# A planner's list of TensorE durations set to traced values, and fillers kept to longer gaps

## The chip, the cores and the metric

The kernel runs on one core of one Trainium2 chip. The metric is the device time of one execution in microseconds; a run's time is that of its slowest core, which here is the only one.

## What is computed

An image batch of shape 8 x 256 x 32 x 32 (8 samples, 256 channels, 1024 positions) goes through four layers:

- Layer 0: a channel norm; attention with 4 heads (key width 32, head width 64) over the 1024 positions; a 3x3 depthwise term and a projection; then a feed-forward part with 1024 hidden channels, 3x3 depthwise convolutions, a gated GELU and a product in the frequency domain of 8x8 patches.
- Layer 1: group norm, attention with 8 heads of width 32 over the same positions, a projection, group norm and a small MLP.
- Layer 2: three convolutions (1x1, 3x3, 1x1) with fake quantization, an addition and a last quantization to codes of 8 bits.
- Layer 3: a selective scan (Mamba) in four directions over the 1024 positions.

The attention of both layers is, cut to what matters:

```
attn = softmax(q^T k * scale)        # 1024 x 1024 for each sample and head
out  = attn applied to v
```

The kernel first needs, for each query, the maximum and the sum of exponentials over 1024 keys. Then it recomputes the scores, subtracts the logarithm of the sum, takes the exponential and multiplies by the values.

## The kernel before

`phase_a` holds layers 0 to 2, `phase_b` holds layer 3. Every operation of both is written as a small object (`_Op`) that a generator, called a strand, yields. Nothing is issued when it is yielded. A planner, `_Order`, holds all strands and keeps a clock of its own for each engine (`order.free`). It repeatedly takes the strand whose next item could start first by that clock (`start`), breaking ties by rank, issues the item and moves the engine's clock on by the item's cost (`run`). A signal between two engines is put at 0.35 us (`LATENCY`). So the order of instructions on every engine is the planner's, and the planner's costs set it. The chip then executes each engine's list in that order; the costs are not seen again.

A strand may yield one operation, a list of operations of one engine that stay together, or a pair of a cost and such a list. `go` turns these into a cost: the operation's own, the sum over the list, or the number that was given. An operation's own cost is in `_Op.__init__`; a float32 matmul with 512 columns costs 1.76 x 0.5 = 0.88 us.

In phase A eight samples go through layers 0 to 2 as one strand each (`sample`), of which about three are under way at once. Each starts further strands:

- `maxima`: two strands (`some`) take two or four PSUM banks at a time, issue two or four score matmuls with 32 rows each that share TensorE's rows, and then for each bank a maximum on VectorE (`tensor_reduce`) and an exponential with a sum on ScalarE. The matmuls are yielded with a cost of 0.9 for two and 1.0 for four.
- `exponentials`: its strands (`step`) take four banks, issue four score matmuls and four with one row block of -1 (`minus`) that subtract the logarithms, at a cost of SCORES = 1.3; ScalarE then takes four exponentials, after each of which a bank comes free. `values` multiplies them by the values, at a cost of 0.9 x (4n/128), where n is 64 in layer 0 and 32 in layer 1: 1.8 and 0.9.
- All other matmuls of the layers (`mm` and the like) are yielded singly or as lists with the sum of their own costs.

There are eight PSUM banks (`bank`) in phase A. While a sample is in `exponentials`, other work may hold three of them (`OTHERS`). DMAs are issued from SP's queue.

Fillers: ahead of each TensorE item `run` calls `fill` with the item's planned start. `fill` looks how long TensorE is free by the plan before that start, counted from when a bank for it is free, and issues one dummy matmul (bf16, constant operands, 512 columns) for each FILL = 0.3 us of that gap. The result is overwritten. A filler goes to a free bank, or to the bank that the next item starts afresh. Fillers have no cost in the plan. They are on the profile's line L1075; all planned operations are on L132, the line of `emit`.

Phase B has a planner of its own, an `_Order` made anew, without fillers.

Of the kernel before, what the change touches and what calls it, by code (L numbers as in the profile page):

```python
# [29 lines left out]
P = 128  # L30
# [138 lines left out]
class _Order:  # L169
# [7 lines left out]
    def __init__(self, nc):  # L177
        self.nc, self.strands, self.n = nc, [], 0
        self.free, self.written, self.read, self.base, self.last = {}, {}, {}, {}, {}
        self.fill = None  # L180

    def add(self, rank, strand):
        self.n += 1
# [4 lines left out]
    def go(self, s, value=None):  # L188
        try:
            r = s[1].send(value)  # L190
            if isinstance(r, _Op):
                r = (r.cost, [r])
            elif isinstance(r, list):
                r = (sum(o.cost for o in r), r)
            s[2] = r
        except StopIteration:
            self.strands.remove(s)
# [63 lines left out]
def phase_a(ctx, tc, i, col, ident, codes):  # L261
# [18 lines left out]
    order = _Order(nc)  # L280
# [249 lines left out]
    def maxima(rank, q, k, rows, done):  # L530

        both = yield from take(stats)
        least, sums = both[:, 0], both[:, 1]
        todo = [(t, j, h) for t in range(NT) for j in range(2) for h in (0, 2)]
        left = [MAXIMA]

        def some():
            while todo:
                yield lambda: not todo or may(2)
                if not todo:  # L540
                    break
                n = 4 if may(4) and not todo[0][2] else 2
                t, j, h = todo.pop(0)
                if n == 4 and todo:
                    todo.pop(0)
                bb = yield from some_banks(n)
                ops = []
                for e in range(n):
                    r = slice(32 * (h + e), 32 * (h + e) + 32)
                    ops.append(  # L550
                        T.matmul(bb[e], lhsT=q[r, t * P : (t + 1) * P], rhs=k[r, hs(j)], start=True, stop=True)
                    )
                yield (0.9 if n == 2 else 1.0, ops)
                for e in range(n):
                    m, s = (x[:, j, t, h + e : h + e + 1] for x in (least, sums))
                    yield V.tensor_reduce(m, bb[e], AX.X, ALU.max, negate=True)
                    yield A.activation(bb[e], bb[e], AF.Exp, bias=m, accum_out=s)
                    back(bb[e])
            left[0] -= 1

        for _ in range(MAXIMA):
            order.add((1, rank), some())
        yield lambda: left[0] == 0 and not making
        making.append(1)
        m, mx, t = (small.tile([P, NT, 4], F32, name=f"mx{e}", tag=f"mx{e}", bufs=2) for e in range(3))
        yield V.tensor_tensor(m, least[:, 0], least[:, 1], ALU.min)
        for j in range(2):
            yield V.tensor_tensor(least[:, j], m, least[:, j], ALU.subtract)
        yield A.activation(least, least, AF.Exp)
        yield V.tensor_tensor(sums, sums, least, ALU.mult)  # L570
        yield V.tensor_tensor(t, sums[:, 0], sums[:, 1], ALU.add)

        y = small.tile([P, NT, 4], F32, name="ln", tag="ln", bufs=2)
        put(stats, both)
        yield A.activation(y, t, AF.Ln)
        yield V.tensor_tensor(mx, y, m, ALU.subtract)
        yield A.activation(y, y, AF.Exp, scale=-1.0)
        yield V.tensor_tensor(t, t, y, ALU.mult)
        yield V.scalar_tensor_tensor(mx, t, -1.0, mx, ALU.add, ALU.add)
        for e in range(2):  # L580
            b = small.tile([P, NT, 4], BF16, name="mb", tag="mb", bufs=2)
            yield V.tensor_copy(b, mx)
            yield V.tensor_copy(parts[:, :, :, e], b)
            yield V.tensor_tensor(mx, mx, parts[:, :, :, e], ALU.subtract)
        yield V.tensor_copy(parts[:, :, :, 2], mx)
        for h in range(2):
            pr = yield from side()
            yield [
                T.transpose(pr[:, t * P : (t + 1) * P], parts[:, 4 * h + t].rearrange("p a b -> p (a b)"), ident)
                for t in range(4)  # L590
            ]
            yield A.copy(rows[:, hs(h)], pr)
            back(pr)
        making.clear()
        done()

    def exponentials(rank, tasks, vt, n, finish):

        yield lambda: not attending
        attending.append(1)
        for task, (h, steps) in enumerate(tasks):
            po = yield from take(bank)
            seen = [0]

            def step(k, four, h=h, seen=seen):
                bb = yield from takes(4, bank, when=lambda: seen[0] >= k - 1)
                ops = []
                for b, (q, kk, rows, key, r, *_) in zip(bb, four):  # L610
                    r4, r3 = slice(r, r + 32), slice(r, r + 3)
                    ops.append(
                        T.matmul(
                            b, lhsT=kk[r4, key * P : (key + 1) * P], rhs=q[r4, hs(h)],
                            start=True, stop=False, skip_group_check=True,
                        )
                    )
                for b, (q, kk, rows, key, r, *_) in zip(bb, four):
                    r3 = slice(r, r + 3)
                    ops.append(  # L620
                        T.matmul(
                            b, lhsT=minus[r3, :], rhs=rows[r3, hs(h)], start=False, stop=True, skip_group_check=True
                        )
                    )
                yield (SCORES, ops)
                tiles = []
                for n in range(2):
                    t = yield from take(exps)
                    for e in range(2):
                        yield A.activation(t[:, e], bb[2 * n + e], AF.Exp)  # L630
                        put(bank, bb[2 * n + e])
                    tiles.append(t)
                order.add((1, rank), values(k, four, tiles))

            def values(k, four, tiles, po=po, seen=seen, last=len(steps) - 1):
                es = [t[:, e] for t in tiles for e in range(2)]
                yield lambda: seen[0] == k
                ops = []
                for e, (q, kk, rows, key, r, c, at) in zip(es, four):
                    ops.append(  # L640
                        T.matmul(
                            po[at : at + n], lhsT=vt[:, key, c : c + n], rhs=e,
                            start=(k == 0 and key == 0), stop=(k == last), skip_group_check=True,
                        )
                    )
                yield (0.9 * (4 * n // P), ops)
                for t in tiles:
                    put(exps, t)
                seen[0] += 1

            for k, four in enumerate(steps):
                order.add((0, rank), step(k, four))
            yield lambda: seen[0] == len(steps)
            order.add((0, rank), finish(task, po))
        attending.clear()
# [397 lines left out]
    def fill(gap, ops):  # L1053


        free, o = order.free.get("tensor", 0.0), ops[0]
        spare = min(bank.left, key=lambda k: order.last.get((bank.tag, k), 0.0), default=None)
        own = o.method == "matmul" and o.kw["start"] and o.args[0].shape[-1] == HALF and o.kw["rhs"].shape[0] > 3
        since = min(
            [order.last.get((bank.tag, k), 0.0) for k in bank.left] + [order.base.get(o.args[0].name, 0.0)] * own,  # L1060
            default=1e9,
        )
        n = int((gap - max(free, since)) / FILL)
        if n < 1:
            return
        if spare is not None and order.last.get((bank.tag, spare), 0.0) <= since:
            bank.left.remove(spare)
            bank.left.insert(0, spare)
            t = bank.take()
        else:  # L1070
            t = None
        out = o.args[0] if t is None else t
        rhs = minus.unsqueeze(1).to_broadcast([P, 4, P])
        for _ in range(n):
            nc.tensor.matmul(out, lhsT=minus[:, : out.shape[0]], rhs=rhs, start=True, stop=True)  # L1075
        if t is not None:
            bank.put(t)

    order.fill = fill
    stage = [0] * B  # L1080

    def sample(b):
# [640 lines left out]
```

## Time and profile before

| what | value |
|---|---|
| runs | 10776.5, 10775.12, 10765.92 us; median 10775.12 |
| profiled execution, its own time | 10771.94 us |
| its span | 10770.2 us |
| mean granted TensorE clock | 0.957 |
| fillers (matmuls on L1075) | 1594, from 1.6 to 3666.7 us |
| ScalarE, exponentials of scores (`exps`) | 1536, 797.4 us busy, mean 621 ns |
| ScalarE, exponentials of maxima (`bank`) | 1536, 1023.0 us busy, mean 669 ns |
| VectorE, maxima (`stats`) | 1536, 981.5 us busy, mean 681 ns |
| VectorE, waiting in front of the maxima for TensorE's banks | 746.4 us |

The span runs from the first to the last instruction; the execution's own time is 1.7 us longer. In rows of the timeline the first number is the start in microseconds, the second the time that the merged instructions took, and "x4" how many there were. A float32 matmul that isn't a transpose appears as two records, so "x8" is four matmuls. In rows of the windows, the columns are the stretch, its length, the busy time of TensorE, its weight loads, VectorE, ScalarE and GpSimd with the count of instructions, the mean granted TensorE clock, the busy share of the DMA engines, and GB/s. Tiles are named without buffer numbers: `bank` is a PSUM bank, `exps` an exponential, `big` a buffer with q, k, v or the like, `minus` a constant of -1.

### The profile page before, as it was taken

The page shows a single profiled execution, that of the slowest core. Times are in us where ns is not written, and L with a number is a line of the kernel's source. Part 1 is how long each engine was busy: PE and PEld are TensorE (multiplying, and loading weights), DVE is VectorE, ACT ScalarE, POOL GpSimd, SP SyncE. Part 2 cuts the span into 40 slices and gives each one's busy share as a digit, 9 for nine tenths or more (in the row PEclk, how much of TensorE's full clock was granted, in tenths as well). Part 3 has the DMA queues.
Part 4 walks back from the last instruction along what each step waited for, and adds up shares of the span by engine and source line. Part 5 has one row for each costly group of instructions (what it writes and reads, how often), then busy time and mean ns, then how long its engine had stood idle before and what let it go on. Part 6 is the DMA issues. An engine that isn't in the chain of part 4 may idle for free. (4 is left out here: it accounts for less than half of the span.)

```text
span 10770.2 us, 157247 instructions
## 1 busy us (share of the span) xinstructions
PE 9924.2 (92%) x58586; PEld 6252.6 (58%) x58698; DVE 8478.2 (79%) x8992; ACT 8690.8 (81%) x16283; POOL 6733.0 (63%) x3745
## 2 busy tenths in 40 slices
PE   9999999999999889999999999999989999999998
PEld 3333333333333267777777777777777777777776
DVE  5266557577665379898998998998899899899897
ACT  7867676777767488888888888888888888888887
POOL 1432133132220178888888888888888888888887
PEclk7988999989999899999999999999999999999999
DMA  1000000000000011111111111111111111111111
GB/s 46 29 18 16 22 16 22 13 22 12 13 13 10 30 41 39 50 48 50 48 46 52 50 41 55 41 50 53 44 49 52 47 48 46 52 50 43 55 41 47
DMA packets 217345, 410.00 MB, mean 38 GB/s; under 512 B 24881, under 2 KB 69297, under 8 KB 211458
## 3 DMA queue, kind: packets, MB, share of 16 engines
q1 hardware_dynamic: 216578, 399.94, 12.0%
q8 instruction: 461, 7.55, 0.3%
q14 instruction: 306, 2.51, 0.1%
HBM read 358.43 MB, written 30.93 MB: 36 GB/s over the span
## 5 line engine op out<-in xcount | busy, mean ns | idle before, releaser
L132 POOL TENSOR_TENSOR h<-h,cb 128x1024 f32<-128x1024 f32 x2048 | 4873.9, 2395 | 899.6 <-ACT st L132 445.5
L132 ACT ACTIVATE da<-dt,am 128x512 f32<-128x512 f32 x4096 | 2869.3, 713 | 505.9 <-DVE h L132 497.4
L132 DVE TENSOR_TENSOR_SCAN h<-da,st,db 128x512 f32<-128x512 f32 x2048 | 2467.2, 1257 | 167.9 <-PE db L132 92.7
L132 DVE TENSOR_TENSOR_SCAN h<-da,db 128x512 f32<-128x512 f32 x2048 | 2346.1, 1198 | 230.7 <-PE db L132 152.0
L132 ACT ACTIVATE dbu<-du,bT 128x512 f32<-128x512 f32 x3584 | 2474.9, 709 | 34.1 <-PE db L132 31.8
L132 PE MATMUL db<-ident,dbu 128*128 128x128 f32 x14336 | 2219.6, 280 | 165.0 <-DVE h L132 134.6
L132 PE MATMUL py<-ident,h 128*128 128x128 f32 x16384 | 2121.1, 275 | 93.9 <-POOL h L132 86.2
L132 PEld LDWEIGHTS db<-ident,dbu 128*128 128x128 f32 x14336 | 1672.9, 143 | 694.4 <-DVE h L132 364.2
L132 PEld LDWEIGHTS py<-ident,h 128*128 128x128 f32 x16384 | 1842.4, 141 | 171.5 <-POOL h L132 140.7
L132 DVE TENSOR_REDUCE stats<-bank 128x1 f32<-128x512 f32 x1536 | 981.5, 681 | 747.5 <-PE bank L132 746.4
L132 ACT ACTIVATE bank<-bank,stats 128x512 f32<-128x512 f32 x1536 | 1023.0, 669 | 391.2 <-DVE stats L132 380.9
L132 POOL TENSOR_TENSOR mid<-mid,mid 128x961 f32<-128x961 f32 (+2 forms) x192 | 401.2, 2097 | 1046.9 <-ACT mid L132 676.9
L132 PE MATMUL pp<-xi,cvd 128*128 128x512 f32 x2048 | 953.3, 609 | 9.6 <-ACT xs L132 3.4
L132 PE MATMUL bank<-big,big 32*128 32x512 f32 x4096 | 908.5, 670 | 36.5 <-ACT bank L132 17.9
L132 ACT ACTIVATE exps<-bank 128x512 f32<-128x512 f32 x1536 | 797.4, 621 | 137.6 <-PE bank L132 133.2
L132 PE MATMUL db<-dg,du 128*128 128x128 f32 x4096 | 811.0, 280 | 0.0
L132 POOL TENSOR_TENSOR dt<-dt,tmp 128x512 f32<-128x512 f32 x512 | 652.0, 1273 | 173.8 <-DVE tmp L132 151.0
L132 DVE TENSOR_TENSOR tmp<-dt,xs 128x512 f32<-128x512 f32 x256 | 604.2, 2360 | 194.3 <-POOL dt L132 194.1
L132 PEld LDWEIGHTS db<-dg,du 128*128 128x128 f32 x4096 | 638.0, 197 | 0.0
L132 PEld LDWEIGHTS pp<-xi,cvd 128*128 128x128 f32 x2048 | 380.8, 196 | 406.4 <-issue 391.9
L132 DVE SCALAR_TENSOR_TENSOR mid<-mid,cols,mid 128x961 f32<-128x961 f32 (+1 forms) x384 | 603.7, 1572 | 6.7
L132 PEld LDWEIGHTS bank<-big,big 32*128 32x128 f32 x4096 | 284.7, 192 | 499.2 <-issue 247.9
(186 smaller groups left out, 11280.3 us busy)
## 6 DMA issues: line engine op xcount, KB each, us to landing
cb<-c_d SPq DMA_DIRECT2D x1024, 256.0 KB, 3.2
wi<-w_in SPq DMA_DIRECT2D x192, 192.0 KB, 3.4
big<-in_x_dram SPq DMA_DIRECT2D x16, 1024.0 KB, 5.6
kept<-big SPq DMA_DIRECT2D x16, 1024.0 KB, 4.0
big<-kept SPq DMA_DIRECT2D x16, 1024.0 KB, 4.9
cdb<-codes SPq DMA_DIRECT2D x48, 256.0 KB, 4.1
big<-big SPq DMA_DIRECT2D x16, 512.0 KB, 7.2
out_dram<-z SPq DMA_DIRECT2D x32, 256.0 KB, 2.5
```

Source lines behind the costliest of these rows:

```text
L132: return getattr(getattr(nc, self.engine), self.method)(*self.args, **self.kw)
```

## The change

It has four parts, all in the planner's data.

1. Maxima: the matmuls are yielded with 1.06, for two as for four banks.
2. Values: the cost is 0.88 x (4n/128) + 0.12, so 1.88 in layer 0 and 1.00 in layer 1.
3. Lists of TensorE operations that come without a given cost get 0.1 us more (`order.way`, 0.1 in phase A, 0.0 in phase B). Single matmuls and items with a given cost don't.
4. `fill` takes 0.35 us off the gap before it divides by 0.3.

```
-        self.fill = None
+        self.fill, self.way = None, 0.0
...
-                r = (sum(o.cost for o in r), r)
+                r = (sum(o.cost for o in r) + self.way * (r[0].engine == "tensor"), r)
...
-                yield (0.9 if n == 2 else 1.0, ops)
+                yield (1.06, ops)
...
-                yield (0.9 * (4 * n // P), ops)
+                yield (0.88 * (4 * n // P) + 0.12, ops)
...
-        n = int((gap - max(free, since)) / FILL)
+        n = int((gap - max(free, since) - 0.35) / FILL)
...
-    order.fill = fill
+    order.fill, order.way = fill, 0.1
```

## The prediction

> **What bounds the kernel now.** I read the page first, to find which part of the span the edits can touch.
>
> ```profile
> span 10770.2 us, 157247 instructions
> PE 9924.2 (92%) x58586; PEld 6252.6 (58%) x58698; DVE 8478.2 (79%) x8992; ACT 8690.8 (81%) x16283; POOL 6733.0 (63%) x3745
> ...
> PE   9999999999999889999999999999989999999998
> ...
> PEclk7988999989999899999999999999999999999999
> ```
>
> Every slice has TensorE busy, so the page alone decides nothing. The granted clock is lower in the first third than after it, and the groups of the fillers' line say where that third ends and what is in it:
>
> ```profile
> L1075 PE MATMUL bank<-minus x1594: 376/379/634, 1.6 to 3666.7; 128*128 128x512 bf16 x193, 128*64 128x512 bf16 x7
> ```
>
> The last of 1594 fillers starts at 3666.7 us. What follows is phase B, some 7,100 us; its planner has no filler and an extra of 0.0. In the two programs as built its instruction order is the same (common tails of 39,555 TensorE, 10,565 ScalarE and 5,740 VectorE instructions). So it moves as a block, and the change is worth what the first 3667 us change.
>
> Inside those I took the TensorE timeline of a stretch that repeats one pattern, then ScalarE's in the same place:
>
> ```profile
> 1060.23 0.61 PE L1075 MATMUL bank<-minus 128*128 128x512 bf16 x2
> 1060.76 1.14 PE L132 MATMUL bank<-big,big 32*128 32x512 f32 x8
> 1061.72 0.40 PE L132 MATMUL bank<-low,minus 3*128 3x512 bf16 x4
> 1062.05 1.07 PE L132 MATMUL bank<-exps,big 128*32 128x512 f32 x8
> 1063.05 1.13 PE L132 MATMUL bank<-big 32*128 32x512 f32 x4
> 1064.11 0.61 PE L1075 MATMUL bank<-minus 128*128 128x512 bf16 x2
> 1064.64 1.14 PE L132 MATMUL bank<-big,big 32*128 32x512 f32 x8
> ```
>
> ```profile
> 1062.14 2.06 ACT L132 ACTIVATE exps<-bank 128x512 f32<-128x512 f32 x4 [0.73 <-PE bank L132]
> 1064.06 0.70 ACT L132 ACTIVATE bank<-bank,stats 128x512 f32<-128x512 f32 x1
> 1064.99 0.66 ACT L132 ACTIVATE bank<-bank,stats 128x512 f32<-128x512 f32 x1
> 1066.02 2.06 ACT L132 ACTIVATE exps<-bank 128x512 f32<-128x512 f32 x4 [0.25 <-PE bank L132]
> ```
>
> Read starts against starts, since matmul ends are modelled. One step takes 3.88 us (1060.76 to 1064.64): scores with their minus rows 1.29, values 1.00, two maxima 1.06, two fillers 0.53. No row has an idle figure, and ScalarE waits for TensorE's banks. The old plan has 1.3, 0.9 and 0.9 for the three real pieces: it sees a hole that the chip fills with real work, and puts fillers into it. Windows over this stretch and three neighbours show the clock's side:
>
> ```profile
> core 0: us, PE busy (x) PEld busy (x) DVE busy (x) ACT busy (x) POOL busy (x), PEclk, DMA share, GB/s
> 934.00:944.00 10.00, 9.54 (x33) 3.52 (x30) 7.96 (x13) 9.38 (x22) 6.40 (x4) 1.00 0.01 2
> 944.20:957.70 13.50, 13.34 (x25) 4.12 (x24) 6.23 (x10) 9.93 (x27) 6.60 (x4) 0.50 0.00 0
> 958.00:988.00 30.00, 29.22 (x98) 10.79 (x98) 28.89 (x42) 25.08 (x71) 0.00 (x0) 1.00 0.00 0
> 1048.00:1100.00 52.00, 52.00 (x349) 14.71 (x345) 18.84 (x40) 45.82 (x108) 2.53 (x2) 1.00 0.00 1
> ```
>
> The clock is either whole or 0.50. The same view in windows of 400 us gives phase A's level (two of nine rows):
>
> ```profile
> 0.00:400.00 400.00, 376.18 (x1470) 131.83 (x1470) 160.59 (x303) 309.29 (x668) 108.75 (x62) 0.85 0.14 40
> 1200.00:1600.00 400.00, 373.88 (x1734) 125.78 (x1736) 254.41 (x326) 310.96 (x661) 112.34 (x54) 0.95 0.07 23
> ```
>
> From 1048 to 1100 TensorE is full and ScalarE is at 45.82 of 52.00 us, 88%: TensorE binds there, fillers included, with ScalarE 12% behind.
>
> **What the Trainium skill says.** TensorE: Matmul & The Clock Gate, Part 1, has the array at half rate by default and at full rate after about 3.4 us of activity; the trace agrees on the two rates (1.00 and 0.50). Its section Why this matters for your kernels allows idle gaps up to about 3 us. The trace is stricter: summing streaming time in steps of 3.4 us, I find 34 of the 59 drops in phase A after a step that was still 60 to 85% used, and steps above 85% followed by none. Back-to-back issue gap (Part 2) gives 512/2.4 + 2.5 = 216 ns for a 512-column matmul; here a lone filler costs 0.32 us (1532.34 to 1532.66) and a pair 0.53, so each further one costs 0.21: agreed. Perfetto Trace Analysis, Identifying the Most-Contended Engine, warns that matmul occupancy is no measure of headroom; the 52.00 of 52.00 above, a seventh of it fillers, is a case.
>
> **The change part by part.** *Costs.* Maxima become 1.06 (trace 1063.05 to 1064.11: 1.06). Values of layer 1 become 1.00 (trace 1.00), of layer 0 1.88 (trace 254.26 to 256.13: 1.87). A list of two 128-row matmuls goes from 1.76 to 1.86 (trace 1514.49 to 1516.40: 1.91). All move towards the trace. The edits cost the chip nothing themselves; they act by the order and by the gaps that the filler sees. The order on every engine differs from its first few dozen instructions on. The real work is the same, but maxima in fours rise from 97 to 111 and in twos fall from 574 to 546. Four row-packed matmuls take no longer than two (1.06), so 14 groups fewer free 14 x 1.06 = 15 us of TensorE. No wait is written in; those that the dependences need are about as many (TensorE 13,820 and 13,775, ScalarE 14,686 and 14,764). No DMA is added, and SP's count is unchanged; a moved DMA is hidden as before (DMA is 3 to 14% busy here); were that cover gone, one load is 5 us.
>
> *Fillers.* The program before has 1594 in 453 runs, the one after 949 in 243. At 0.32 for the first of a run and 0.215 for others that is 453 x 0.32 + 1141 x 0.215 = 390 us against 243 x 0.32 + 706 x 0.215 = 230 us: 160 us of TensorE issue go. Not all of it stood in the way. For each of the 453 runs I compared its start with the end of the last instruction that frees a bank or makes an input for the group after it, plus 0.15 us for the signal. 97 runs (196 fillers) began when that group was ready; they cost 67 us. With the other runs whose group came before the fillers' end, all fillers together delayed real work by 137 us. That is the ceiling of removal. The steps of the pattern above (four values, two maxima, nothing else) lose most: 129 fillers in 86 steps become 27 in 91.
>
> How much of 137 goes? In the pattern a step falls from 3.88 to at best 3.35 on TensorE, and ScalarE needs 4 x 0.477 + 2 x 0.67 = 3.25 (starts in dense runs), with its small operations 0.88 x 3.88 = 3.4: about 0.45 of 0.53 comes out, and then ScalarE is next. But 11 full-clock steps of this kind that have no filler average 4.0 us (least 3.59), so not every step will reach that. I take 60% of 137: 82 us, plus about two thirds of the 15 us of grouping: 10 us.
>
> *Threshold.* A planned gap under 0.65 us now stays empty, and longer ones keep 0.35 us: where the gap is real, idle TensorE. By the nine windows of 400 us to 3600 the clock was 0.85, 0.90, 0.93, 0.95, 0.93, 0.91, 0.95, 0.91, 0.93, so 0.74 x 400 x 2 = 592 us ran at half rate. TensorE is over 90% busy, so a half-rate microsecond costs about 0.45. Bounds: none more (dropped fillers sat in false gaps) to +300 us (half as much again), that is 0 to 135 us of loss. A gain is possible too, if a denser order leaves fewer thin steps: perhaps 30 us. I take +60 us at half rate: 27 us lost.
>
> Sum: -82 - 10 + 27 = -65 us. On the profiled execution 10771.94 - 65 = 10707; the median of the runs is 3.2 us above it, so 10710 us.
>
> **Rivals.** *The clock (slower).* The 0.35 us left open makes enough 3.4 us steps thin that half rate spreads. It beats the 92 us of gain from about 205 us of new half-rate time on, an average clock of 0.89 where it was 0.92. At +330 us it loses 150 us: 10775 - 92 + 150, about 10835. For it: steps just above the limit are common, and fillers are what lifts them. Against it: where fillers were false, TensorE stays full without them.
>
> *ScalarE and the bank ring (no change).* Freed TensorE time turns into waiting for banks, as in the 4.0 us steps without fillers: of 82 us some 30 remain, the clock takes 25 back: about 10770.
>
> *A better plan (more).* With planned and real times in step, the new order also removes waits that are not fillers: TensorE was idle 174 us in the first 3600 (sum of the same windows). All 137, 15 and a fifth of that idle time: 10775 - 187, about 10590 to 10640.
>
> That the edits do nothing is excluded: the programs differ in 645 matmuls.
>
> **How the numbers follow.** Forecast case (10650 to 10753) 0.53; better plan (below 10650) 0.08; no change (10754 to 10797) 0.17; clock (above) 0.22. A measurement of this kernel tells about 0.2%, 21 us, from none. Faster 0.61, same 0.17, slower 0.22. The range leaves out some 0.08 below 10640 and 0.11 above 10830, the far half of the clock case; the forecast's own is 10650 to 10753.
>
> **What would show it.** After: fillers 949; phase A's last matmul at about 3600; the pattern step at 3.4 to 3.6 us with ScalarE over 92% in it; phase B as long as before; mean clock in phase A 0.90 to 0.92. Wrong if the step still takes 3.9 us with idle TensorE before the scores (no change), or if the clock falls under 0.89 there (slower).

## The result and the profile after

The changed kernel takes 10732.95 us, the median of 5 runs from 10712.72 to 10736.98; the kernel before takes 10775.12 beside it (5 runs, 10751.72 to 10783.01). The ratio is 0.9961, with a 95% interval from 0.9946 to 0.9976: 42 us faster, where 65 were forecast; by the interval the gain is 26 to 58 us. The page of the changed kernel:

```profile
span 10735.2 us, 155993 instructions
PE 9872.1 (92%) x57941; PEld 6286.0 (59%) x58053; DVE 8489.3 (79%) x8995; ACT 8687.5 (81%) x16280; POOL 6739.8 (63%) x3742
...
PE   9999998999999789999999989999999999999997
...
PEclk7988998999898899999999999999999999999999
...
L132 DVE TENSOR_REDUCE stats<-bank 128x1 f32<-128x512 f32 x1536 | 985.7, 684 | 711.8 <-PE bank L132 710.4
```

The engines' busy shares are the same to a per cent, so they would not show that anything happened. VectorE's wait for TensorE's banks ahead of the maxima is 710.4 us, 36 less than before. The fillers' line (min, median and longest duration in ns, then the first and last start) tells where the time went:

```profile
L1075 PE MATMUL bank<-minus x949: 376/379/634, 1.6 to 3617.8; 128*128 128x512 bf16 x178, 128*64 128x512 bf16 x12
```

The last filler starts 49 us earlier. From here on "phase A" is the time to the last matmul that writes a `bank`, read to within a microsecond: 3667.3 us before, 3618.6 after. Phase B's main part, from its first `db` matmul to the end, is the same instructions in both: 6961 and 6976 us, and 6958 to 6976 in all 14 profiles of this study. So a phase's length in one profile moves by some 10 us either way without any change of the kernel. Part of that goes with the clock, whose time at half rate after phase A ranges from 287 to 379 us in these profiles. The 35 us between the two spans are 49 gained in phase A less 14 of such scatter.

The TensorE timeline of the changed kernel, in a stretch with the step of the forecast:

```profile
1568.89 0.39 PE L1075 MATMUL bank<-minus 128*128 128x512 bf16 x1
1569.21 1.18 PE L132 MATMUL bank<-big,big 32*128 32x512 f32 x8
1570.17 0.43 PE L132 MATMUL bank<-low,minus 3*128 3x512 bf16 x4
1570.54 1.06 PE L132 MATMUL bank<-exps,big 128*32 128x512 f32 x8
1571.53 1.13 PE L132 MATMUL bank<-big 32*128 32x512 f32 x4
1572.21 1.31 PE L132 MATMUL bank<-big,big 32*128 32x512 f32 x7
...
1576.03 0.39 PE L1075 MATMUL bank<-minus 128*128 128x512 bf16 x1
1576.35 1.14 PE L132 MATMUL bank<-big,big 32*128 32x512 f32 x8
```

Two steps take 7.14 us (1569.21 to 1576.35), 3.57 each, with one filler for both; before, one took 3.88 with two fillers. From 1571.53 to 1572.21 is less than the 1.06 us that two maxima take elsewhere: they and the next scores even overlap. The stretch shown is better than the mean. Over all such steps at full clock (four scores, four values, two maxima and nothing else but fillers), the mean is 3.89 us in 55 before and 3.62 us in 60 after. That is some 16 us in all, a third of the gain; the rest lies elsewhere. The windows say who is next:

```profile
core 0: us, PE busy (x) PEld busy (x) DVE busy (x) ACT busy (x) POOL busy (x), PEclk, DMA share, GB/s
1562.30:1584.00 21.70, 21.70 (x151) 7.50 (x149) 7.21 (x13) 20.95 (x50) 0.00 (x0) 1.00 0.00 1
```

ScalarE is at 20.95 of 21.70 us, 97%, where it was at 88%. The clock's side, two rows of the windows of 400 us:

```profile
0.00:400.00 400.00, 376.13 (x1467) 143.34 (x1469) 175.26 (x313) 324.92 (x693) 127.35 (x70) 0.84 0.14 40
1200.00:1600.00 400.00, 380.14 (x1639) 132.23 (x1639) 255.90 (x316) 321.39 (x686) 107.33 (x51) 0.91 0.07 23
```

The nine windows to 3600 us give 0.84, 0.91, 0.87, 0.91, 0.92, 0.92, 0.92, 0.93 and 0.93, a mean of 0.906 where it was 0.918. By the clock records phase A ran 692.9 us at half rate; before it was 587.1.

### The profile page after: what moved, and what is told of

It reads as the page before. It is cut to its first block, busy times and chain, and to the rows that moved or that the text cites. A ratio compares the mean times of both kernels' runs of the same rounds, so it can differ in the third digit from the quotient of the medians.

```text
span 10735.2 us, 155993 instructions
## 1 busy us (share of the span) xinstructions
PE 9872.1 (92%) x57941; PEld 6286.0 (59%) x58053; DVE 8489.3 (79%) x8995; ACT 8687.5 (81%) x16280; POOL 6739.8 (63%) x3742
## 5 line engine op out<-in xcount | busy, mean ns | idle before, releaser
L132 DVE TENSOR_REDUCE stats<-bank 128x1 f32<-128x512 f32 x1536 | 985.7, 684 | 711.8 <-PE bank L132 710.4
L132 PE MATMUL bank<-big,big 32*128 32x512 f32 x4096 | 981.1, 684 | 42.5 <-ACT bank L132 37.6
L132 PEld LDWEIGHTS bank<-big,big 32*128 32x128 f32 x4096 | 335.9, 196 | 523.9 <-issue 199.5
L132 POOL TENSOR_SCALAR big<-big,ga,gs 128x512 f32<-128x512 f32 x64 | 63.0, 997 | 909.8 <-DVE gs L132 686.3
```

The source lines that it names most:

```text
L132: return getattr(getattr(nc, self.engine), self.method)(*self.args, **self.kw)
```

## The experiments

The change mixes two things: another order (from the durations) and fewer fillers (from the threshold, and because the new plan has fewer gaps). My theory was that dropped fillers, those in false gaps (gaps of the plan that the chip does not have), give the gain and the clock takes part of it back. The rivals were that the new order gives it, or that fillers hardly matter. Two numbers are read from each trace. "Half rate" is the time in phase A at a granted clock of 0.5. "Delay" is the sum over all runs of fillers of how long they kept the group of matmuls after them waiting when its banks and inputs were ready (with 0.15 us allowed for the signal): 137 us before, 75 after.

### One order, three filler counts

The first two kernels keep the old order, instruction for instruction, and change only how many fillers `fill` issues: those that the new rule leaves, or none.

```
old_order_fewer, in the kernel before:
-        for _ in range(n):
+        for _ in range(int((gap - max(free, since) - 0.35) / FILL)):
old_order_none, in the kernel before, and new_order_none, in the changed kernel:
-        for _ in range(n):
+        for _ in range(0):
costs_only, in the changed kernel:
-        n = int((gap - max(free, since) - 0.35) / FILL)
+        n = int((gap - max(free, since)) / FILL)
```

`costs_only` and `new_order_none` have the changed kernel's order in the same way, but for the numbers of the banks.

Every ratio below is to the kernel before as it was timed beside that kernel, on the same chip. Its median was 10778.04 us beside the four kernels here, 10783.33 beside `way_011`, `scores_129`, `act_cost` and `tight_fill`, and 10774.48 beside the last four further on. So ratios can be compared across the tables, and medians only roughly. Phase A, half rate and delay come from one profiled execution of each kernel.

old_order_fewer: 

> The old order on every engine, instruction for instruction, with the fillers that the new rule leaves: 1102 instead of 1594. If the dropped fillers stood in the way (forecast), this alone gives about half of the change's gain: 10745 us. If the gain is the new order's, this gains nothing, and loses through the clock: 10775 to 10795 us, with over 640 us at half rate in the layers before the scan, where the kernel before had 587.

costs_only: 

> The new durations without the new threshold: the order of the changed kernel (bank numbers apart), with 1373 fillers instead of 949. If the order carries the gain, it is as fast as the changed kernel or faster, 10715 to 10735 us, with less time at half rate than 693 us. If the fillers that the threshold drops stand in the way, it keeps half of the gain: 10750 us.

new_order_none: 

> The order of the changed kernel with no fillers. If fillers hold the clock, half rate before the scan rises from 693 to 900 us or more and the time to 10780 to 10830 us. If they mostly delay work (75 us of delay by the trace after), it falls to about 10690 us.

old_order_none: 

> The order of the kernel before with no fillers. If fillers hold the clock: half rate from 587 to 950 us or more, which costs about 165 us against at most 137 us of delay that goes: 10790 to 10850 us. If they mostly delay: 10690 us.

| kernel | order | fillers | phase A, us | half rate, us | delay, us | median, us | ratio (95%) |
|---|---|---|---|---|---|---|---|
| before | old | 1594 | 3667.3 | 587.1 | 137 | 10775.12 | 1 |
| old_order_fewer | old | 1102 | 3633.6 | 692.9 | 69 | 10740.05 | 0.9961 (0.9947 to 0.9975) |
| old_order_none | old | 0 | 3661.9 | 1097.9 | 0 | 10768.58 | 0.9992 (0.9983 to 1.0001) |
| costs_only | new | 1373 | 3622.3 | 553.0 | 107 | 10729.82 | 0.9956 (0.9939 to 0.9972) |
| after | new | 949 | 3618.6 | 692.9 | 75 | 10732.95 | 0.9961 (0.9946 to 0.9976) |
| new_order_none | new | 0 | 3641.9 | 1043.9 | 0 | 10747.75 | 0.9971 (0.9961 to 0.998) |

The fillers' lines of the two kernels with one part each:

```profile
L1075 PE MATMUL bank<-minus x1102: 376/379/634, 1.6 to 3632.5; 128*128 128x512 bf16 x175, 128*64 128x512 bf16 x9
```

```profile
L1075 PE MATMUL bank<-minus x1373: 376/379/634, 1.6 to 3621.7; 128*128 128x512 bf16 x187, 128*64 128x512 bf16 x10
```

What follows:

- Fewer fillers in the old order are as good as the whole change (0.9961 both). Nothing moved in that kernel but fillers, so it is shown that in this order fillers stood in the way. I had expected about half of the gain from it.
- The durations alone are as good as the whole change too (0.9956), which is the reading that I had set down for the order. The two parts don't add up: the new durations already take out part of the false gaps (1373 fillers, delay 107), and the threshold in the new order gains 3.7 us of phase A, within the scatter. So in the changed kernel's own order no run shows that the 424 fillers dropped by the threshold were worth anything in all; what they gave and cost there is worked out below.
- Without fillers the clock falls. Two rows of `old_order_none`, and the same two of the kernel before:

```profile
1600.00:2000.00 400.00, 353.88 (x1388) 141.70 (x1388) 264.80 (x378) 282.83 (x616) 111.47 (x56) 0.84 0.06 20
2000.00:2400.00 400.00, 353.21 (x1366) 145.70 (x1359) 264.69 (x348) 258.88 (x559) 113.58 (x56) 0.87 0.05 18
```

```profile
1600.00:2000.00 400.00, 376.10 (x1601) 144.22 (x1597) 270.28 (x384) 281.24 (x613) 111.79 (x56) 0.93 0.06 20
2000.00:2400.00 400.00, 370.99 (x1555) 140.06 (x1556) 264.98 (x348) 265.68 (x574) 112.05 (x56) 0.91 0.05 18
```

0.93 becomes 0.84 and 0.91 becomes 0.87, and yet the kernel is no slower: 511 us more at half rate cost what 137 us of delay had cost. My expectation of 10790 to 10850 us was wrong; so was 10780 to 10830 for the new order, which came out at 10747.75.

Two prices explain the three lengths of the old order. Let a microsecond of delay cost a, and one at half rate b. From `old_order_fewer`, -33.7 = -69a + 105.8b; from `old_order_none`, -5.4 = -137a + 510.8b. Hence a = 0.81 and b = 0.21 with the delays before rounding (0.80 and 0.20 with the rounded ones). Two equations for two unknowns leave nothing over to test them with, and 5 us of scatter in each length would move a by up to 0.15 and b by up to 0.05. For the new order, counted from `costs_only`, they give +3 us for the changed kernel (measured -4) and +15 for `new_order_none` (measured +20): within the scatter of one profile.

The record holds a second price, and it is higher. Executions of one unchanged kernel differ in their granted clock, and time goes with it: in the 35 of the kernel before with the median 10774.48, a mean clock of 0.960 went with 10750 us (6 executions) and one of 0.956 with 10784 (3). A line through all 35 gives 0.34 us for each microsecond at half rate, and through the 26 with the median 10778.04 it gives 0.36. That is a correlation over the whole span. It can't replace 0.21 here: with 0.35 the old order would need a = 1.02 in the first equation and 1.34 in the second. So half-rate time that missing fillers cause was cheap in this phase, and 0.21 is no price of the clock in general. Why the two differ is open.

### Other draws of the order

A planner of this kind reorders nearly everything when one number moves. So the order's share may be luck: one draw, so to say, out of many orders. Four of these kernels change a cost that hardly matters, in the changed kernel or in the one before. Two take one part of the durations alone. `act_cost` sets one more number to the trace, and `tight_fill` tries the two prices on the order that is already known.

```
way_011, in the changed kernel:
-    order.fill, order.way = fill, 0.1
+    order.fill, order.way = fill, 0.11
scores_129, in the changed kernel; old_scores_129 and old_scores_131, in the kernel before:
-    MAXIMA, SCORES = 2, 1.3
+    MAXIMA, SCORES = 2, 1.29            (1.31 in the last)
act_cost, in the changed kernel:
-            self.cost = 0.05 + 0.87 * n + (0.1 if len(ins) > 1 else 0)
+            self.cost = 0.05 + 0.87 * n + (0.1 if len(ins) > 1 else 0) + (0.09 if "accum_out" in kw else 0)
tight_fill, in the changed kernel:
-    FILL = 0.3
+    FILL = 0.215
maxima_only: the change's first part alone, old threshold
lists_only: the change's third part alone, old threshold
```

way_011: 

> The changed kernel with 0.11 instead of 0.1 for lists: durations as true as before, another order from the 111th TensorE instruction on, 880 fillers. If the new order's share of the gain comes from true durations, the layers before the scan stay within 10 us of 3619. If it is one draw among many orders, they may end anywhere within some 40 us, up to where they were, 3667 us.

scores_129: 

> The changed kernel with 1.29 instead of 1.3 for the scores (1.29 is what the trace shows): a second draw, 985 fillers. Same two readings: within 10 us of 3619 before the scan, or anywhere up to 3667.

act_cost: 

> The changed kernel with 0.09 us more for each exponential with a sum: planned 0.585, starts in dense runs are 0.67 apart in the trace. If a truer plan pays by itself, this gains again: 3600 us before the scan, 10715 us in all. If what paid was that false gaps went, it gains nothing more: within 10 us of the changed kernel or of its neighbours.

tight_fill: 

> The order of the changed kernel (bank numbers apart); a gap still loses 0.35 us, but what is left is filled at 0.215 us a filler, as the trace has them, not 0.3: 1502 fillers. By the four runs before, a microsecond of delay by fillers costs 0.81 and one at half rate 0.21. If that holds: half rate falls from 693 to about 580 us (gain 24 us) and delay rises from 75 to about 100 us (loss 20 us): no change, 3610 to 3622 us before the scan. If the number of fillers is what costs, it loses 30 us.

old_scores_129: 

> The kernel before with 1.29 instead of 1.3 for the scores: the old durations and the old rule in another order (from the 461st TensorE instruction on), 1695 fillers. If the order of the kernel before was one bad draw, the layers before the scan end well below 3667 us, at 3620 to 3640. If the old durations cost time in any order, they end within 12 us of 3667.

old_scores_131: 

> The kernel before with 1.31 for the scores: a second draw with the old durations, 1641 fillers. Same two readings: 3620 to 3640 us before the scan if the order before was a bad draw, within 12 us of 3667 if the old durations cost time in any order.

lists_only: 

> Of the new durations only the 0.1 us for lists; old rule, 1506 fillers, of which 172 in 105 steps of the common kind (before 129 in 86). The false gaps of these steps remain, so by the forecast's reading this gains little: 3650 to 3670 us before the scan. If the gain is from a truer plan of the other matmuls, 3630 us.

maxima_only: 

> Of the new durations only the maxima's; old rule, 1462 fillers, of which 132 in 97 steps of the common kind. Values are still planned 0.1 short, so false gaps remain in part: 3640 to 3660 us before the scan. If the maxima's cost is what matters, 3620 us, as with all new durations.

Three profiled executions are poor stand-ins for their medians: that of `lists_only` was the slowest of its six, 20 us above the median, that of `old_scores_129` the slowest of its 14, 30 us above, and that of `way_011` the slowest of its six, 14 us above. The others lie within 10 us of theirs. In the next table "rest" is what is left of the change of phase A against the kernel before, once 0.81 x delay and 0.21 x half rate are taken off.

| kernel | durations | fillers | phase A, us | half rate, us | delay, us | rest, us | median, us | ratio (95%) |
|---|---|---|---|---|---|---|---|---|
| old_scores_129 | old | 1695 | 3673.9 | 566.6 | 138 | +10 | 10766.71 | 0.9994 (0.9986 to 1.0003) |
| old_scores_131 | old | 1641 | 3681.2 | 580.3 | 143 | +10 | 10789.54 | 1.0018 (1.0008 to 1.0027) |
| maxima_only | in part | 1462 | 3668.8 | 645.1 | 146 | -18 | 10771.18 | 1.0 (0.9992 to 1.0009) |
| lists_only | in part | 1506 | 3642.2 | 549.5 | 136 | -16 | 10724.4 | 0.9957 (0.9943 to 0.9971) |
| costs_only | new | 1373 | 3622.3 | 553.0 | 107 | -14 | 10729.82 | 0.9956 (0.9939 to 0.9972) |
| after | new | 949 | 3618.6 | 692.9 | 75 | -21 | 10732.95 | 0.9961 (0.9946 to 0.9976) |
| tight_fill | new | 1502 | 3625.5 | 529.1 | 122 | -17 | 10735.62 | 0.9958 (0.9943 to 0.9973) |
| way_011 | new | 880 | 3611.6 | 699.7 | 71 | -26 | 10712.23 | 0.9938 (0.9924 to 0.9953) |
| scores_129 | new | 985 | 3609.8 | 692.9 | 64 | -20 | 10714.58 | 0.9936 (0.9921 to 0.9951) |
| act_cost | new, and ScalarE's | 1008 | 3631.1 | 737.3 | 79 | -20 | 10730.53 | 0.9953 (0.9938 to 0.9968) |

The fillers' lines show the ends of phase A: first of a draw with the new durations, then of one with the old:

```profile
L1075 PE MATMUL bank<-minus x985: 376/379/634, 1.6 to 3609.0; 128*128 128x512 bf16 x184, 128*64 128x512 bf16 x13
```

```profile
L1075 PE MATMUL bank<-minus x1641: 376/379/634, 1.6 to 3680.7; 128*128 128x512 bf16 x177, 128*64 128x512 bf16 x6
```

and of the two kernels with one part of the durations, `lists_only` first:

```profile
L1075 PE MATMUL bank<-minus x1506: 376/380/636, 1.6 to 3641.6; 128*128 128x512 bf16 x183, 128*64 128x512 bf16 x6
```

```profile
L1075 PE MATMUL bank<-minus x1462: 376/380/635, 1.6 to 3668.3; 128*128 128x512 bf16 x173, 128*64 128x512 bf16 x10
```

- Three orders with the old durations end phase A at 3667 to 3681 us, three with all the new ones and the new rule at 3610 to 3619. The first three have the old rule for fillers too, so this compares both parts of the change at once. With the old rule and the new durations there is one order, `costs_only`, and it ends at 3622, 45 us ahead of the best of the three. So the order before was no bad draw: the old durations cost time in each of the three orders tried. Among orders of one kind the draw is worth up to some 15 us.
- The best two, `way_011` and `scores_129`, beat both kernels (0.9938 and 0.9936). Each was meant as a change too small to matter. That one is better than the changed kernel beyond a draw isn't shown.
- `tight_fill` fits the prices: 47 us more delay and 164 us less half rate than in the changed kernel should cost 4 us; phase A is 7 us longer (I had expected a delay of 100 us and 580 at half rate; 122 and 529 came). The difference is within the scatter, so the test is a weak one; a = 1.02 with b = 0.35 would make phase A 9 us shorter. That the number of fillers by itself costs is refuted: 1502 cost no more than 949.
- `act_cost` fell short. A planned 0.675 us for ScalarE's exponentials with sums, which fits the trace, was to gain 20 us and gained none (3631.1). So this order gives no support to the reading that a truer plan pays in general. It is one draw.
- For the two parts alone I expected the reverse of what came. The lists' 0.1 us gains 25 us of phase A in its profile with its delay unchanged (136 us), and the maxima's cost gains nothing. By the timed runs the lists do more: 0.9957, as much as the whole change, with 1506 fillers kept. Its common steps still take 3.95 us in the mean (75 at full clock). So one part of the durations, in one order, gives the whole gain without removing the false gaps. As its profile was its slowest execution, its rest of -16 is likely too small by some 20 us. `maxima_only` has a rest of -18 by the two prices, and loses it to 58 us more at half rate and 9 of delay.

What makes the rest is not settled. Fewer maxima in twos, as the forecast had it, is not it: `lists_only` issues more pairs than the kernel before (690 for 684) and still gains.

## Why the prediction was right, point by point

**What binds, and where.** Right. Phase B moved as a block, and the gain lies before 3667 us.

**False gaps.** Right as a cause, too large in size. The pattern step went from 3.88 to 3.57 us in the stretch shown, with ScalarE next at 97%, as said. The cause is shown in the old order; in the new one its share is worked out with the prices. The term "60% of 137" was 82 us of delay to go. The trace after has 75 us left, so 62 went, and at 0.81 each that is 50 us. The threshold leaves more fillers in the way than I took it to: in `old_order_fewer`, which has it alone, half of the delay stays.

**Grouping.** I put 10 us on fewer maxima in twos, and that step was wrong. The counts of 97 and 111 fours took two neighbouring pairs on different rows for a four. The planner issued 42 fours before and 46 after, and 684 and 676 pairs: four groups fewer, some 4 us and not 15. Where maxima of all four row groups stood in a row with nothing beside them, at full clock, 27 of 59 such stretches took under 1.3 us before and 17 of 31 after. The order has a share, 14 to 26 us by the rests of the kernels with all new durations, but not for that reason. That it makes up in part for what the false gaps fell short is luck.

**Threshold and clock.** Two errors that nearly cancel, which is luck. The term was 60 us more at half rate at 0.45 each, 27 us. It was 106 us, at 0.21 each: 22 us. The time at half rate rose beyond what I took; that it did so because 0.35 us stay empty ahead of every remaining run fits `costs_only` (553.0 us without that rule, 692.9 with it). The price was too high because I took it from TensorE's busy share, as if each microsecond there were on the path. In the Trainium skill, TensorE: Matmul & The Clock Gate, Terms puts the penalty at half the time at half rate (1 - 4/8); in six kernels here, which differ in fillers alone within each order, less than half of that reaches the end, and over executions of one unchanged kernel about 0.7 of it (0.34 to 0.36). That the clock falls mostly where TensorE waits for others anyhow would explain it, but it is only argued; in phase A of the kernel before, TensorE was busy for 90% of the time at half rate and for 96% of the rest, which is no great difference.

**The sum.** -50 + 22 and about -21 of the order make -49 us in phase A, against -65 forecast. The -21 is a remainder, so the sum had to come out. Fillers and clock together gave about -28 us where -55 was forecast; with the higher prices (1.02 and 0.35) they give -26. So the number landed in its range with half of the net gain that I put on fillers and clock, and with an order's share that has another reason than mine.

**The rivals.** The slower one, by the clock, is refuted. Its point of decision, about 205 us of new half-rate time, was worked out with 0.45; `old_order_none` has 511 us more and is not slower. ScalarE and the bank ring do come next, but after most of the step's gain, not ahead of it. The better plan exists in part (the rest), at an eighth of the idle time of 174 us, not the whole case. `lists_only` shows that it can be worth more than that: its gain of 0.43% came with the delay unchanged in its profile.

## What to carry to other kernels

A dummy instruction that fills a planned gap is free only if the gap exists on the chip: compare the planner's durations with starts in the trace, and for each filler the moment when the work behind it was ready. Weigh the clock by experiment, with the order held fixed and the fillers at three counts; here a microsecond of delay was worth about four at half rate. Judge an order by several draws, made by changes too small to matter themselves, ahead of crediting one number of a cost table, since the draw alone is worth 0.1% or more. Take lengths of one profile for what they are: look how far the profiled execution lies from the median.

## What the runs showed of the hardware

The granted clock fell after moderate idleness: in phase A of the kernel before, 34 of 59 drops came after a 3.4 us step in which TensorE was still streaming for 60 to 85% of the time, and none after a step above 85%. Not every such step brought a drop: of those at 80 to 85% with the clock whole, 5 of 113 did. Without any fillers phase A ran 1044 to 1098 us of some 3650 at half rate, and lost 23 to 28 us to the best filler count of its order. Two and four score matmuls of 32 rows, packed into TensorE's rows, took nearly the same time in the kernel before: a pair 1.06 us (1063.05 to 1064.11), and four 1.08:

```profile
1930.38 1.14 PE L132 MATMUL bank<-big 32*128 32x512 f32 x8
1931.46 0.82 PE L1075 MATMUL bank<-minus 128*128 128x512 bf16 x3
```

So a pair alone costs twice as much for each bank; where other scores overlap it, as at 1571.53 after, it costs less.
